# Square roots by a power instruction on GpSimd instead of ScalarE roots with Newton steps

## The chip, the cores and the metric

The kernel runs on one core of one Trainium2 chip. A core has five engines with instruction queues of their own: TensorE (matmuls; PE, and PEld for the load of its weights), VectorE (DVE), ScalarE (ACT), GpSimd (POOL) and SyncE (SP, which here only issues DMAs). They meet through semaphores. The metric is the device time of one execution in microseconds.

## The reference

Two layers over `x` (64 x 256 x 256) with one adjacency matrix `adj` (256 x 256), each a layer norm, a ReLU, a graph network and a residual sum:

```python
# layer 0
h = jnp.maximum(_layernorm(x), 0.0)
x = x + _L0_gnn_ref(h, adj, adj, W1, W2, W3)      # three products with adj*adj, widths 512, 1024, 256
# layer 1
h = jnp.maximum(_layernorm(x), 0.0)
x = x + _L1_gnn_ref(h, adj, V1, b1, V2, b2)
# inside layer 1
deg = A.sum(0) + A.sum(1) - diag(A)
d = where(deg > 0, rsqrt(deg), 0)
_, U = eigh(d[:, None] * (diag(deg) - A) * d[None, :])
out = relu((U.T @ features) @ V1 + b1) @ V2 + b2
return U @ out
```

`_layernorm` is `(x - mean) / sqrt(var + 1e-5)`. Layer 1 needs all eigenvectors of one symmetric 256 x 256 matrix, the same for the whole batch. Layer 0 doesn't depend on them.

## The kernel before, in words

**Two works at once.** The eigenvectors are one long serial chain (class `Eigen`), mostly small VectorE instructions. Layer 0 (class `Layers`) is mostly matmuls, over 32 pairs of batch entries. The kernel writes both into one program: the chain's instructions in their order, and between them, from two streams of layer-0 instructions (`products` and `rows`), whatever fits.

**The planner.** Class `Pace` decides what fits. Every call on an engine becomes an `Op`, which carries an estimate of how long it occupies its engine (`busy`, lines 107 to 120) and when its result is there (`until`). For a chain instruction, `chain` (line 211) works out when its inputs will be ready and first emits stream instructions that start before that. The order on PE and ACT is thus fixed when the program is written; a chain instruction on PE stands behind the layer-0 matmuls that the planner put in front of it, and those behind it wait if it isn't ready. Estimates of the chain are multiplied by 1.06 (1.13 in the blocks of reflections). The order on VectorE and GpSimd is left to the framework's scheduler.

**The chain's stages.** `laplacian` (402) makes the normalised matrix, with `d` from one root. `tridiagonalize` (439) takes 254 Householder steps. A step works on rows and columns from `lo` on; up to `lo` = 127 it handles two row halves of A, after that one. Each step has the same frame: `below` copies the leading entry (`alpha`) and sums the squares of the rest on ScalarE (`tail`; in the second half on VectorE); `length` (483) forms `nn` = x1*x1 + tail, takes its root `s0` on ScalarE, and forms a sign `q` and `qn`; the next step then needs `rs` = 1/s0, `qs` = q*s0, and `nb` = rs*qn + qs, which is the signed length with a Newton step on the root. `nb` (its tile is called m in the profile) goes into `ac`, whose transposes on PE (psB) start the rest of the step; `none`, made on GpSimd, goes into `den` a few instructions later. Between `nn` and `nb` VectorE updates A with two products per half (lines 559 to 561). `aside` puts single-column helpers on GpSimd in the first half and on VectorE in the second.

Then come the leaves (QL steps on 16 x 16 blocks, which keep their ScalarE roots in both versions), with the reflections put together in blocks on PE, and four levels of divide and conquer (`level`, 1280). A level takes six roots of `dq` in `rational_steps` (1189), and two with a Newton step by the helper `root` (349): of `zp` at line 1674, and of `nrm` at 1688. A root by `root` is five instructions: ScalarE Sqrt, then reciprocal, product, sum and halving on VectorE.

**The norms.** `norm` (1811) runs 65 times, for 64 half-works of a pair and once more because the first pair is split in two. Per run ScalarE sums the four parts of x, VectorE makes the mean `nm`, ScalarE sums the squares, and then VectorE (variance), ScalarE (root) and VectorE (five instructions: a Newton step, `scale`, `shift`) finish before ScalarE's `relu_norm` uses scale and shift.

**The end.** When the chain is done, a flag says whether a repair is needed (`mend`, 1726): the register read of it is followed by a branch. `go_on` puts 3.5 us of layer-0 work before it, and 4.5 us after it while layer 1's first rows load. Layer 1 (`layer1`, 2107) takes 32 items through three products each; what is left of layer 0 is filled in between its instructions, and at item 8 `finish` emits all the rest at once. The pairs 30 and 31 come as items 11 and 12. The transposes of pair 31's normed rows (`turn_rows`) are held back until item 8.

Of the kernel before, what the change touches and what calls it, by code (L numbers as in the profile page):

```python
# [27 lines left out]
N = 256  # L28
# [54 lines left out]
class Op:  # L83
# [4 lines left out]
    def __init__(self, part, call, args, kwargs):  # L88
        self.part, self.engine, self.call, self.args, self.kwargs = part, ENGINES[part], call, args, kwargs
        self.name = call.__name__  # L90
        free = lambda a: int(np.prod([int(n) for n in a.shape[1:]]))
        named = dict(kwargs)
        outs = [named.pop("out")] if "out" in named else [args[0]]
        ins = [a for a in [*(args if "out" in kwargs else args[1:]), *named.values()] if isinstance(a, bass.AP)]
        total = named.pop("accum_out", None)
        if isinstance(total, bass.AP):
            outs.append(total)
            ins = [a for a in ins if a is not total]
        self.outs, self.ins = [span(a) for a in outs], [span(a) for a in ins]
        n = max(free(a) for a in outs[:1] + ins) if self.engine == "DVE" else free(outs[0])  # L100
        sums = len(outs) > 1

        if self.engine == "PE":
            self.columns = 0 if "transpose" in self.name else n
            self.busy = max(n * self.COLUMN, 0.224) if self.columns else 0.115
            self.until = max(self.busy, 0.165) + 0.35
        elif self.engine == "ACT":
            pointers = any(isinstance(kwargs.get(k), bass.AP) for k in ("scale", "bias"))
            self.busy = 0.13 + n / 1400 + 0.12 * pointers + 0.19 * sums
            self.until = self.busy + 0.12  # L110
        elif self.engine == "DVE":
            each = 6.3 if self.name == "reciprocal" else 2.0 if self.name == "tensor_tensor_scan" else 1.0
            pointers = self.name == "scalar_tensor_tensor" or any(a.shape[1:] == [1] for a in ins[1:])
            self.busy = 0.065 + 0.06 * pointers + each * n / 960 + 0.08 * sums
            self.until = self.busy + 0.125
        elif self.engine == "POOL":
            self.busy = 0.2 + 2 * n / 960
            self.until = self.busy + 0.1
        else:
            self.busy, self.until = 0.1, 4.0  # L120
# [160 lines left out]
class Eigen:  # L281


    def __init__(self, tc, ctx, ap, gt2, pace):
# [117 lines left out]
    def laplacian(self):  # L402
# [13 lines left out]

        safe, rt, tmp = self.col("c3"), self.col("c4"), self.col("c5")
# [21 lines left out]
    def tridiagonalize(self, a):  # L439
# [24 lines left out]
        row = lambda tag: self.sp.tile([P, N], F32, tag=tag, name=tag)  # L464
        guard = self.col("guard", 1)
        nc.vector.memset(guard, 1e-30)
        book = self.mat("m1")
# [15 lines left out]
        def length(xr, lo, tail):  # L483

            nn, s0, q, qn = (self.col(c, 1) for c in ("nn", "s0", "q", "qn"))
# [5 lines left out]
            return nn, s0, q, qn  # L491

# [4 lines left out]
        alpha, tail = below(xr, 1)  # L497
        nn, s0, q, qn = length(xr, 1, tail)
        for k in range(N - 2):
# [5 lines left out]

            rs, qs, nb = self.col("rs", 1), self.col("qs", 1), nbs[:, k : k + 1]
# [56 lines left out]
            if more:  # L563
                alpha, tail, (nn, s0, q, qn) = alpha1, tail1, following

# [623 lines left out]
    def rational_steps(self, n, kd, zsum, zown, znxt, acc, s, gap, half, y, bs, rb):  # L1189
# [33 lines left out]
        for step in range(ROOT_STEPS):  # L1223
# [40 lines left out]
            self.ts(dq, dq, 1e-36, OP.max)  # L1264
            nc.scalar.activation(dq, dq, AF.Sqrt)
            self.tt(b, b, dq, OP.add)
# [13 lines left out]
    def level(self, n, qt, dc, rho, sg, bad=None):  # L1280
# [452 lines left out]
class Layers:  # L1733


    def __init__(self, tc, ctx, ap, gt2, u, ut):
# [74 lines left out]
    def norm(self, x, scale, shift, parts=range(4)):  # L1811
# [3 lines left out]
        at = slice(parts[0], parts[-1] + 1, parts[1] - parts[0])  # L1815
        s, nm, v, tmp = (self.sp.tile([P, g], F32, tag=c, name=c) for c in ("s", "nm", "v", "tmp"))
        for j in parts:
            junk = self.sp.tile([P, N], F32, tag="junk", name="junk", bufs=1)
            yield nc.scalar.activation(junk, x[:, j // 2, j % 2, :], AF.Copy, accum_out=s[:, j : j + 1])
        yield nc.vector.tensor_scalar(nm[:, at], s[:, at], -1.0 / N, None, OP.mult)  # L1820
        for j in parts:
            junk = self.sp.tile([P, N], F32, tag="junk", name="junk", bufs=1)
            yield nc.scalar.activation(
                junk, x[:, j // 2, j % 2, :], AF.Square, bias=nm[:, j : j + 1], accum_out=v[:, j : j + 1]
            )
        s, nm, v, tmp, scale, shift = (t[:, at] for t in (s, nm, v, tmp, scale, shift))
# [371 lines left out]
```

## Time and profile before

| | us |
|---|---|
| median of 3 runs (range) | 2428.49 (2427.74 to 2430.24) |
| profiled execution, span | 2426.6 |
| PE busy | 2381.5 |
| VectorE busy | 2127.2 |
| ScalarE busy | 1013.8 |
| GpSimd busy | 480.6 |
| ScalarE root of nn, 254 times | 74.5 |
| ScalarE root of v (norms), 65 times | 13.2 |
| the seven VectorE instructions of the norms, 65 times each | 78.0 |

Almost every instruction is emitted from one line of the planner (L209 in the first part, L213 after the planner's end), so groups are told apart by the tiles that they write and read and not by lines. Where the program has put several names into one place of memory, the profile shows one of them: `nb` is m, the tridiagonal form's `uc` is q, its partial products are r, `gam` is z. A matmul in 32-bit floats appears as two rows. Instructions of one engine overlap in the profile: the start of the next one, not the end of the last, tells what one costs in a chain. In the answers "idle before" is the time in which the engine stood still ahead of an instruction, with what ended it behind the arrow.

### The profile page before, as it was taken

What the parts mean: (1) busy time and instruction counts of PE and PEld (TensorE: products, weight loads), DVE (VectorE), ACT (ScalarE), POOL (GpSimd) and SP (SyncE); (2) the same over time, 40 slices, a digit from 0 to 9 for tenths busy, and PEclk for the clock granted to TensorE, in tenths of its full rate; (3) what the DMA queues carried; (4) which work ended last, traced back from release to release, by engine and by line L of the source; (5) the groups of instructions that cost most, each with busy time, mean ns of one, the idle gap of its engine ahead of it and who ended that gap; (6) DMA issues with size and microseconds to landing.
All of it is one profiled execution on the core that took longest, in us unless ns stands there. A gap on an engine that the chain in (4) does not pass through costs nothing. (4 is left out here: it accounts for less than half of the span.)

```text
span 2426.6 us, 38393 instructions
## 1 busy us (share of the span) xinstructions
PE 2381.5 (98%) x9226; PEld 1581.7 (65%) x9226; DVE 2127.2 (88%) x12971; ACT 1013.8 (42%) x2827; POOL 480.6 (20%) x1752
## 2 busy tenths in 40 slices
PE   7999999999999999999999899999999999999999
PEld 4666666666666566666666666666566666666788
DVE  8999999999999999999999989999997888886443
ACT  4444454444444444344444244344344434443322
POOL 2334333343333111111111000000000000000443
PEclk9999999999999999999999999999999999999999
DMA  3000000000000000000000000000000000000676
GB/s 113 18 21 7 23 23 18 23 23 23 6 23 23 18 22 23 22 6 23 23 23 26 10 23 23 23 23 22 18 22 27 22 23 12 16 22 1 210 255 204
DMA packets 59399, 90.02 MB, mean 37 GB/s; under 512 B 5792, under 2 KB 42784, under 8 KB 59168
## 3 DMA queue, kind: packets, MB, share of 16 engines
q1 hardware_dynamic: 59168, 87.52, 10.8%
q8 instruction: 74, 1.21, 0.2%
q14 instruction: 157, 1.29, 0.2%
HBM read 47.13 MB, written 40.37 MB: 36 GB/s over the span
## 5 line engine op out<-in xcount | busy, mean ns | idle before, releaser
L209 PE MATMUL bank<-y,L_gnn_W 128*128 128x512 f32 (+2 forms) x2182 | 903.5, 566 | 1.1 <-ACT y L209 1.1
L209 PEld LDWEIGHTS bank<-y,L_gnn_W 128*128 128x128 f32 x2182 | 401.8, 190 | 440.7 <-issue 419.0
L209 PE MATMUL bank<-L_gnn_W,s 128*128 128x256 f32 (+1 forms) x2092 | 465.2, 375 | 3.2 <-ACT s L209 3.2
L209 PEld LDWEIGHTS bank<-L_gnn_W,s 128*128 128x128 f32 x2092 | 386.7, 190 | 52.2 <-ACT s L209 3.9
L209 ACT ACTIVATE s<-bank 128x512 f32<-128x512 f32 x384 | 224.9, 586 | 196.4 <-PE bank L209 196.0
L209 PE MATMUL bank<-gt,s 128*128 128x256 f32 x1036 | 233.7, 379 | 2.8 <-ACT s L209 2.8
L209 PE MATMUL bank<-L_gnn_W,y 128*128 128x512 f32 (+2 forms) x542 | 230.9, 569 | 1.1 <-ACT y L209 1.1
L209 PEld LDWEIGHTS bank<-gt,s 128*128 128x128 f32 x1036 | 194.7, 191 | 39.7 <-issue 10.5
L209 ACT COPY y<-bank 128x512 f32<-128x512 f32 x192 | 111.5, 582 | 138.9 <-PE bank L209 138.6
L209 PEld LDWEIGHTS bank<-L_gnn_W,y 128*128 128x128 f32 x542 | 100.2, 190 | 97.3 <-issue 91.1
L209 POOL COPY m<-xr 128x1 f32<-128x1 f32 x254 | 55.8, 220 | 534.5 <-DVE xr L209 526.5
L209 ACT ACTIVATE s<-nn,guard 128x1 f32<-128x1 f32 x254 | 74.5, 293 | 208.1 <-DVE nn L209 169.0
L209 ACT ACTIVATE h<-x,shift,scale 128x256 f32<-128x256 f32 x256 | 137.3, 589 | 54.6 <-DVE shift L209 54.4
L209 ACT ACTIVATE junk<-x 128x256 f32<-128x256 f32 x256 | 105.6, 412 | 95.8 <-DVE x L209 80.5
L209 ACT ACTIVATE junk<-x,nm 128x256 f32<-128x256 f32 x256 | 129.0, 504 | 37.1 <-DVE nm L209 32.6
L209 DVE SCALAR_TENSOR_TENSOR A<-xr,wc,A 128x255 f32<-128x255 f32 (+63 forms) x381 | 139.9, 368 | 0.0
L209 DVE SCALAR_TENSOR_TENSOR A<-wr,q,A 128x255 f32<-128x255 f32 (+63 forms) x381 | 138.9, 366 | 0.0
L209 ACT ACTIVATE junk<-xr 128x254 f32<-128x254 f32 (+63 forms) x127 | 46.0, 362 | 216.5 <-DVE xr L209 211.4
L209 DVE SCALAR_TENSOR_TENSOR q<-q 128x1 f32<-128x1 f32 (+1 forms) x576 | 119.8, 208 | 13.0 <-ACT q L209 2.3
L209 PE MATMUL bank<-gt,h 128*128 128x256 f32 (+1 forms) x518 | 120.6, 382 | 0.1
L209 POOL TENSOR_TENSOR xb<-x,ub 128x512 f32<-128x512 f32 x16 | 19.9, 1271 | 495.5 <-DMA hw<-hw 485.6
L209 PE MATMUL bank<-p,gt 128*128 128x512 f32 (+2 forms) x270 | 117.0, 570 | 0.1
(615 smaller groups left out, 4306.2 us busy)
## 6 DMA issues: line engine op xcount, KB each, us to landing
x<-x SPq DMA_DIRECT2D x60, 512.0 KB, 3.6
x<-in_x_dram SPq DMA_DIRECT2D x64, 256.0 KB, 3.7
out_dram<-out SPq DMA_DIRECT2D x64, 256.0 KB, 2.2
hw<-hw SPq DMA_DIRECT2D x60, 256.0 KB, 2.7
L_gnn_W<-in_L_gnn_W_dram SPq DMA_DIRECT2D x1, 2048.0 KB, 10.9
L_gnn_W<-in_L_gnn_W_dram SPq DMA_DIRECT2D x1, 1024.0 KB, 13.5
L_gnn_W<-in_L_gnn_W_dram SPq DMA_DIRECT2D x1, 512.0 KB, 6.3
mask<-in_c_blk_dram SPq DMA_DIRECT2D x2, 256.0 KB, 3.1
```

The costliest lines, as they stand in the source:

```text
L209: return op.call(*op.args, **op.kwargs)
```

## The change

A tile of constants 0.5 and -0.5 is set once, and a helper raises a tile to that power on GpSimd. It replaces ScalarE's Sqrt and the steps around it in the front (`laplacian`), in the tridiagonal form, in `rational_steps` and at the two places in `level`; in the norms of both layers the variance, the power and the shift are all made on GpSimd, and the mean comes straight from ScalarE's scaled sum. The planner gets a price for the power. The roots in the leaves stay as they are.

```diff
         elif self.engine == "POOL":
-            self.busy = 0.2 + 2 * n / 960
+            power = OP.pow in args
+            self.busy = 0.2 + (0.14 * n + 0.15 if power else 2 * n / 960)
...
+        self.powers = {0.5: pool.tile([P, H], F32, name="half"), -0.5: pool.tile([P, H], F32, name="less")}
+        for y, t in self.powers.items():
+            tc.nc.vector.memset(t, y)
...
+    def power(self, out, a, y):
+        return self.nc.gpsimd.tensor_tensor(out, a, self.powers[y][:, 0 : out.shape[-1]], OP.pow)
...
-        self.root(rt, safe, tmp)
-        dinv = self.col("c6")
-        self.recip(dinv, rt)
+        self.power(dinv, safe, -0.5)
...
             self.stt(nn, x1, x1, tail, OP.mult, OP.add)
-            nc.scalar.activation(s0, nn, AF.Sqrt, bias=guard)
+            self.power(s0, nn, 0.5)
             aside(lo).tensor_scalar(q, x1, 0.0, 0.5, OP.is_ge, OP.subtract)
-            aside(lo).tensor_tensor(qn, q, nn, OP.mult)
...
-            self.recip(rs, s0)
-            aside(lo).tensor_tensor(qs, q, s0, OP.mult)
...
                 if h == halves[0]:
-                    self.stt(nb, rs, qn, qs, OP.mult, OP.add)
+                    self.stt(nb, q, 2.0, s0, OP.mult, OP.mult)
...
         self.ts(dq, dq, 1e-36, OP.max)
-        nc.scalar.activation(dq, dq, AF.Sqrt)
+        self.power(dq, dq, 0.5)
...
-        self.recip(zp, zp)
-        self.root(zh, zp, tmp)
+        self.power(zh, zp, -0.5)
...
-        self.root(rn, nrm, tmp)
-        self.recip(rn, rn)
+        self.power(rn, nrm, -0.5)
...
+        self.rsqrt = pool.tile([P, 2 * H], F32, name="rsqrt")
+        self.nc.vector.memset(self.rsqrt, -0.5)
...
-            yield nc.scalar.activation(junk, x[:, j // 2, j % 2, :], AF.Copy, accum_out=s[:, j : j + 1])
-        yield nc.vector.tensor_scalar(nm[:, at], s[:, at], -1.0 / N, None, OP.mult)
+            yield nc.scalar.activation(
+                junk, x[:, j // 2, j % 2, :], AF.Copy, scale=-1.0 / N, accum_out=nm[:, j : j + 1]
+            )
...
-        yield nc.vector.tensor_scalar(v, v, 0.25 / N, 0.25 * LN_EPS, OP.mult, OP.add)
-        yield nc.scalar.activation(s, v, AF.Sqrt)
-        yield nc.vector.reciprocal(tmp, s)
-        yield nc.vector.tensor_tensor(tmp, tmp, v, OP.mult)
-        yield nc.vector.tensor_tensor(s, s, tmp, OP.add)
-        yield nc.vector.reciprocal(scale, s)
-        yield nc.vector.tensor_tensor(shift, nm, scale, OP.mult)
+        yield nc.gpsimd.tensor_scalar(v, v, 1.0 / N, LN_EPS, OP.mult, OP.add)
+        yield nc.gpsimd.tensor_tensor(scale, v, self.rsqrt[:, 0 : scale.shape[-1]], OP.pow)
+        yield nc.gpsimd.tensor_tensor(shift, nm, scale, OP.mult)
```

More of the change, by code (lines that the diff above doesn't have):

```diff
@@ L415, in laplacian @@
         self.tt(deg, deg, dg, OP.subtract)
-        safe, rt, tmp = self.col("c3"), self.col("c4"), self.col("c5")
+        safe, dinv = self.col("c3"), self.col("c6")
         self.ts(safe, deg, 1e-30, OP.max)
-        self.root(rt, safe, tmp)
-        dinv = self.col("c6")
-        self.recip(dinv, rt)
+        self.power(dinv, safe, -0.5)
         self.stt(dinv, deg, 0.0, dinv, OP.is_gt, OP.mult)
@@ L464, in tridiagonalize @@
         row = lambda tag: self.sp.tile([P, N], F32, tag=tag, name=tag)
-        guard = self.col("guard", 1)
-        nc.vector.memset(guard, 1e-30)
         book = self.mat("m1")
@@ L483, in length @@
         def length(xr, lo, tail):
-            nn, s0, q, qn = (self.col(c, 1) for c in ("nn", "s0", "q", "qn"))
+            nn, s0, q = (self.col(c, 1) for c in ("nn", "s0", "q"))
             x1 = xr[:, lo : lo + 1]
             self.stt(nn, x1, x1, tail, OP.mult, OP.add)
-            nc.scalar.activation(s0, nn, AF.Sqrt, bias=guard)
+            self.power(s0, nn, 0.5)
             aside(lo).tensor_scalar(q, x1, 0.0, 0.5, OP.is_ge, OP.subtract)
-            aside(lo).tensor_tensor(qn, q, nn, OP.mult)
-            return nn, s0, q, qn
+            return nn, s0, q
         xc = self.col("xc")
@@ L497, in tridiagonalize @@
         alpha, tail = below(xr, 1)
-        nn, s0, q, qn = length(xr, 1, tail)
+        nn, s0, q = length(xr, 1, tail)
         for k in range(N - 2):
@@ L504, in tridiagonalize @@
             rc = a[:, :, lo]
-            rs, qs, nb = self.col("rs", 1), self.col("qs", 1), nbs[:, k : k + 1]
-            self.recip(rs, s0)
-            aside(lo).tensor_tensor(qs, q, s0, OP.mult)
+            nb = nbs[:, k : k + 1]
             xa, junk = self.col("xa"), self.row("r0")
@@ L563, in tridiagonalize @@
             if more:
-                alpha, tail, (nn, s0, q, qn) = alpha1, tail1, following
+                alpha, tail, (nn, s0, q) = alpha1, tail1, following
         done = slice(0, N - 2)
@@ L1264, in rational_steps @@
             self.ts(dq, dq, 1e-36, OP.max)
-            nc.scalar.activation(dq, dq, AF.Sqrt)
+            self.power(dq, dq, 0.5)
             self.tt(b, b, dq, OP.add)
@@ L1815, in norm @@
         at = slice(parts[0], parts[-1] + 1, parts[1] - parts[0])
-        s, nm, v, tmp = (self.sp.tile([P, g], F32, tag=c, name=c) for c in ("s", "nm", "v", "tmp"))
-        for j in parts:
-            junk = self.sp.tile([P, N], F32, tag="junk", name="junk", bufs=1)
-            yield nc.scalar.activation(junk, x[:, j // 2, j % 2, :], AF.Copy, accum_out=s[:, j : j + 1])
-        yield nc.vector.tensor_scalar(nm[:, at], s[:, at], -1.0 / N, None, OP.mult)
+        nm, v = (self.sp.tile([P, g], F32, tag=c, name=c) for c in ("nm", "v"))
         for j in parts:
@@ L1823, in norm @@
             yield nc.scalar.activation(
-                junk, x[:, j // 2, j % 2, :], AF.Square, bias=nm[:, j : j + 1], accum_out=v[:, j : j + 1]
+                junk, x[:, j // 2, j % 2, :], AF.Copy, scale=-1.0 / N, accum_out=nm[:, j : j + 1]
             )
-        s, nm, v, tmp, scale, shift = (t[:, at] for t in (s, nm, v, tmp, scale, shift))
-        yield nc.vector.tensor_scalar(v, v, 0.25 / N, 0.25 * LN_EPS, OP.mult, OP.add)
-        yield nc.scalar.activation(s, v, AF.Sqrt)
-        yield nc.vector.reciprocal(tmp, s)
-        yield nc.vector.tensor_tensor(tmp, tmp, v, OP.mult)
-        yield nc.vector.tensor_tensor(s, s, tmp, OP.add)
-        yield nc.vector.reciprocal(scale, s)
-        yield nc.vector.tensor_tensor(shift, nm, scale, OP.mult)
+        for j in parts:
+            junk = self.sp.tile([P, N], F32, tag="junk", name="junk", bufs=1)
+            yield nc.scalar.activation(
+                junk,
+                x[:, j // 2, j % 2, :],
+                AF.Square,
+                bias=nm[:, j : j + 1],
+                accum_out=v[:, j : j + 1],
+            )
+        nm, v, scale, shift = (t[:, at] for t in (nm, v, scale, shift))
+        yield nc.gpsimd.tensor_scalar(v, v, 1.0 / N, LN_EPS, OP.mult, OP.add)
+        yield nc.gpsimd.tensor_tensor(scale, v, self.rsqrt[:, 0 : scale.shape[-1]], OP.pow)
+        yield nc.gpsimd.tensor_tensor(shift, nm, scale, OP.mult)
     def relu_norm(self, x, scale, shift, h, parts=range(4)):
```

## The prediction

> **What bounds the kernel now.** The page first: the span, the busy shares, and the chain that ended last.
>
> ```profile
> span 2426.6 us, 38393 instructions
> PE 2381.5 (98%) x9226; PEld 1581.7 (65%) x9226; DVE 2127.2 (88%) x12971; ACT 1013.8 (42%) x2827; POOL 480.6 (20%) x1752
> PE 7%; DVE 0%; ACT 0%; issue 0%; ACTq 0%; DVEq 0%
> ```
>
> TensorE is busy 98% of the span. The chain of waits names 7% only, since it breaks off where the flag is read; the rest must come from stages. The view of busy time by stage, cut where the work changes (columns: PE, PEld, DVE, ACT, POOL busy, then clock, DMA share, GB/s):
>
> ```profile
> 0.00:20.00 20.00, 8.56 (x23) 5.51 (x24) 10.45 (x63) 9.85 (x29) 1.81 (x10) 1.00 0.92 307
> 20.00:1322.00 1302.00, 1291.02 (x5083) 839.23 (x5082) 1250.31 (x7895) 590.43 (x1711) 391.66 (x1645) 1.00 0.06 20
> 1322.00:1390.00 68.00, 58.82 (x289) 46.56 (x288) 61.67 (x400) 14.98 (x34) 0.45 (x2) 0.97 0.05 16
> 1390.00:2240.00 850.00, 843.98 (x3011) 535.82 (x3009) 730.72 (x4505) 350.66 (x963) 6.76 (x31) 1.00 0.06 20
> 2240.00:2256.00 16.00, 13.31 (x51) 9.01 (x50) 4.75 (x10) 4.40 (x14) 2.87 (x3) 1.00 0.42 148
> 2256.00:2427.00 171.00, 165.77 (x776) 145.51 (x776) 69.26 (x101) 43.49 (x78) 77.04 (x62) 1.00 0.67 224
> ```
>
> Row two is the tridiagonal form: VectorE is busy 96% and TensorE 99%, at once. Row four (leaves and levels) keeps TensorE at 99% with VectorE at 86%. Busy matmuls are modelled, so I checked by columns: 24 matmuls of 256 columns take 5.13 us in the timeline at 506 us, 1,198 columns per us. All matmul rows kept apart by shape hold 2.825 million columns: 2354 us at 1,200 per us. **Only 72 us of the span are not matmul columns**: some 20 at the start, 13 between 1300 and 1400 (the blocked reflections), 6 between 2200 and 2300, 4 at the end, 29 spread thinly. The change removes no matmul, so it can win only out of these.
>
> The second fact is where layer 0 ends. The eigenvectors' chain on VectorE gives its last wide result at 2235 us; the last products of pair 31 run at 2247 to 2249, and what follows is layer 1. **Both queues of work run out together.** A shorter chain leaves layer 0's matmuls to be done afterwards, at the same cost; a longer one leaves TensorE with nothing to fill. The chain is worth nothing when shortened and its full length when lengthened.
>
> The third is the coupling. TensorE's order is fixed when the program is written, by the planner's estimate of the chain. In 20 to 1322 us TensorE waits for VectorE at the chain's transposes (psB) 7.6 us in 15 of 254 steps, VectorE for them 6.5 us in 22 (the views of waits). If a step gets shorter by less than the planner thinks, TensorE waits at every transpose and that time is lost.
>
> **Part by part.** How one step's root stands now, in the second half of the steps (timeline, VectorE alone):
>
> ```profile
> 1002.67 0.21 DVE L209 SCALAR_TENSOR_TENSOR nn<-xr,m 128x1 f32<-128x1 f32 x1
> 1002.81 0.15 DVE L209 TENSOR_TENSOR xc<-xc,lower 128x1 f32<-128x1 f32 x1
> 1002.88 0.29 DVE L209 SCALAR_TENSOR_TENSOR A<-wr,q,A 128x80 f32<-128x80 f32 x1
> 1003.09 0.15 DVE L209 TENSOR_TENSOR qn<-q,nn 128x1 f32<-128x1 f32 x1
> 1003.21 0.30 DVE L209 SCALAR_TENSOR_TENSOR A<-xr,wc,A 128x80 f32<-128x80 f32 x1
> 1003.42 0.16 DVE L209 RECIPROCAL rs<-s 128x1 f32<-128x1 f32 x1
> 1003.50 0.14 DVE L209 TENSOR_TENSOR qs<-q,s 128x1 f32<-128x1 f32 x1
> 1003.55 0.23 DVE L209 SCALAR_TENSOR_TENSOR r<-A,xr 128x79 f32<-128x79 f32 x1
> 1003.71 0.08 DVE L209 DVE_READ_ACCUMULATOR r<-A,xr 128x1 f32 x1
> 1003.71 0.22 DVE L209 SCALAR_TENSOR_TENSOR m<-rs,qn,qs 128x1 f32<-128x1 f32 x1
> ```
>
> *The price of a power.* No row has one. It cannot be cheaper than a POOL product of one column (gg, 195 ns beside little, qs 375 ns beside the updates of A); from above I allow 1 us, where a step's cover ends (below). I take 0.5 us for one column, nearer to the product's rows than to the upper end, and for wider ones the slope that the diff writes into the planner, 0.14 us a column: 0.63 for two, 0.9 for four. The slope is the code's claim and no measurement; few powers are wide, so little hangs on it.
>
> *Second half (127 steps).* qn, rs and qs go: starts of 0.12, 0.08 and 0.05 us, 0.25 together. nn ends at 1002.88; a power of 0.5 from 1002.93 ends at 1003.43, and m could start at 1003.46, where VectorE arrives. Early steps gain up to 0.25; in the last ones (1309 us) nn to m takes 0.85 us with narrow updates between, which no longer cover the power, and they gain nothing. Average 0.1: 13 us.
>
> *First half (127 steps).* rs goes (0.08), and so does the wait for qs: at 504 us m starts at 504.89 because POOL ends qs at 504.86, while VectorE was free at 504.71. The power starts near 503.66 and, even stretched to 0.75 us, ends before 504.63, where m then stands. `none`, queued behind it on POOL and needed by den at 505.0, just fits. 0.26 x 127 = 33 us. What hides the power is the four updates of A, 0.31 us each; a power above 1 us would lose that cover.
>
> *Norms (65).* Seven VectorE instructions go, 78.0 us busy and about 26 us of waits (v 13.2, nm 9.7, tmp 3.5); back to back they fill about half their length, so some 60 us of the chain. POOL gets three, about 0.25 + 0.91 + 0.2 = 1.4 us each time, in order with the tridiagonal helpers; the first waits for ScalarE's sums, and alpha, `none` and the power of a step would wait behind it. VectorE does the same waiting today, so I charge nothing net.
>
> *Levels and front.* 24 roots of dq: rb waited 26.9 us for them, 1.1 each; a power of 0.63 plus hops is 0.8: 7 us. Eight roots with Newton steps: 1.2 us each (2226.06 to 2227.16) become 0.75: 4 us. In the front, c waits 10.23 to 11.90 for root and steps; a power of 0.63 ends near 10.85, so psC starts 0.8 us sooner; the first h waits for v, power and shift until about 12.1 in place of 12.45. Start: 0.7 us.
>
> *Two memsets and 94 us less on ScalarE* (254 x 293, 65 x 206 ns and the small ones) cost and bring nothing: ScalarE is 42% busy.
>
> The chain is thus some 33 + 13 + 60 + 7 + 4 = 117 us shorter on VectorE. **Hardly any of it reaches the end.** What does: the start, 0.7; about half of TensorE's 7.6 us at the transposes, 3.5, since VectorE now runs ahead of the plan by the norms' time; and the gap at 2240 to 2256, where TensorE is idle 2.7 us while flag and first rows arrive, which left-over layer-0 products now fill. Sum 6.9. Span 2426.6 - 6.9 = 2419.7; the median of the runs lies 1.9 us above the profiled span, so **2421.6 us**.
>
> **The rule that speaks against it.** The Trainium skill (SBUF — State Buffer, Who interferes with whom) says that a GpSimd instruction that reads SBUF and a VectorE instruction with two SBUF inputs take one port pair in turn, the later one fully blocked for the whole instruction of the other. The trace shows it where POOL's instruction is long: under xb (1.27 us), v takes 1067 ns against a median of 164. Small ones hardly block: gc takes 0.26 us where gg runs beside it and 0.21 elsewhere; updates of A are at most 0.01 longer beside a POOL instruction. By the row a power costs VectorE 0.05 us a step, 13 us in all, less than is removed; by the rule it holds the pair for its 0.5, some 127 us over 254 steps, more than is removed. A power reads one column and computes; I take the row, and keep the rule as a rival.
>
> **Rivals.**
>
> *The power holds the port.* Place: between nn and m in each step, before an update of A. Price: the 0.3 us by which it exceeds a product, plus 0.05. First half 0.35 - 0.08 = 0.27 x 127 = 34 us, second half 0.35 - 0.25 = 0.10 x 127 = 13 us. The planner knows nothing of it, so TensorE waits: 2421.6 + 47 = **2468 us**. It decides from a hold of about 0.13 us on. For it: xb's row and the rule; against it: gg and the A rows.
>
> *The last pair is caught in the open.* Layer 1's first eight items put about one waiting layer-0 product before each of their own some 84, at about 0.55 us on average 46 us, plus the two fills of 3.5 and 4.5. If more than some 50 us are left when the chain ends, pair 31's norm falls at the end of the forced finish, where TensorE has nothing else: 2.5 us of squares, 1.1 of copies, 1.7 on POOL, 2.1 of relu and 0.8 for the addition are 8 us idle: 2421.6 + 8 = **2430 us**. Today the norm is hidden beside layer 1 (its transposes start at 2290.70 with no gap).
>
> *The chain was the bound after all.* Then its time counts down to the columns plus the start and tail, about **2385 us**. Against it: 99% busy TensorE through 850 us of levels.
>
> *The order comes out differently*, or a first power waits for something that no row shows: about 2440.
>
> **Numbers.** Forecast 0.45, last pair 0.20, port 0.27, chain 0.03, order 0.05. A measurement of this kernel tells 0.2%, 4.9 us, from no change; the forecast is 6.9 away, so 0.35 of its 0.45 are faster and 0.10 same. Faster: 0.35 + 0.03 = 0.38. Same: 0.10 + 0.18 = 0.28. Slower: 0.34. The range takes the forecast with its 10 us of scatter and most of the port's cost: 2411 to 2466; the likeliest case alone, 2414 to 2428.
>
> **What would show it.** Right: matmul columns unchanged; the levels end some 50 to 100 us sooner; TensorE's waits for xr and ac at psB fall to near nothing; layer-0 products stand among the layer-1 ones after the flag; powers of 0.4 to 0.6 us. Wrong: updates of A lengthened by 0.3 us beside a power (port); psB waits in most of the 254 steps (plan); an idle TensorE of 8 us before the last transposes of h (last pair). A power above 1 us would overturn the forecast.

## The result, and the profile after

| | before | after |
|---|---|---|
| median (range), us | 2428.58 (2427.74 to 2430.24) | 2439.59 (2437.77 to 2443.25) |
| ratio, 95% interval | | 1.0048 [1.0036, 1.0060] |
| span of the profiled execution | 2426.6 | 2436.2 |

The change makes the kernel 0.5% slower. VectorE has 110 us less to do and ScalarE 73 us less, and TensorE's matmuls are the same. First the page of the changed kernel: its span, the busy time of each engine, and the chain that ended last.

```profile
span 2436.2 us, 36959 instructions
...
PE 2382.1 (98%) x9216; PEld 1579.2 (65%) x9216; DVE 2016.9 (83%) x11965; ACT 941.0 (39%) x2475; POOL 672.0 (28%) x1980
...
PE 8%; DVE 0%; ACT 0%; issue 0%; ACTq 0%
```

As before, the chain of waits breaks off where the flag is read and decides nothing. Next the changed kernel by stage, with the cuts that the prediction used (busy time of PE, PEld, DVE, ACT, POOL, then clock, DMA share and GB/s).

```profile
0.00:20.00 20.00, 8.55 (x24) 5.22 (x24) 8.95 (x50) 9.95 (x28) 4.52 (x15) 1.00 0.92 308
20.00:1322.00 1302.00, 1277.91 (x5047) 833.51 (x5046) 1175.48 (x7172) 514.11 (x1389) 516.96 (x1753) 1.00 0.06 20
1322.00:1390.00 68.00, 61.40 (x273) 42.29 (x272) 63.68 (x444) 22.86 (x62) 3.59 (x9) 1.00 0.04 12
1390.00:2240.00 850.00, 842.79 (x2985) 532.48 (x2984) 701.35 (x4203) 344.23 (x906) 65.91 (x137) 1.00 0.06 21
2240.00:2256.00 16.00, 16.00 (x75) 12.92 (x74) 1.38 (x2) 3.79 (x7) 9.87 (x8) 1.00 0.64 240
```

In the tridiagonal form (row two) TensorE is busy 1277.9 us where it was 1291.0, although VectorE has 75 us less to do there. The gap around 2240 us is filled: TensorE is busy 16.00 of 16.00 us where it was 13.31.

**Lost time by stage.** The matmul rows, summed over the whole span by shape, hold 2,798,338 columns in both kernels: 2331.9 us at the prediction's rate of 1,200 a microsecond. TensorE thus spends 94.7 us without columns before and 104.3 after, and this 9.6 us is the whole difference of the spans. The same sum for each stage, its length less its columns, gives the table on which the rest stands. (Matmuls at a cut count on both sides, so a row adds up to some 3 us too little.) "First" is 20 to 760 us, "second" from there to the last step, "reflections" up to the first leaf, then leaves and levels up to the flag.

| lost us | start | first | second | reflections | leaves, levels | end |
|---|---|---|---|---|---|---|
| before | 14.7 | 21.1 | 14.2 | 8.0 | 22.9 | 10.8 |
| after | 14.2 | 24.3 | **27.5** | 4.9 | 22.2 | 7.9 |
| e2_norms_back | 13.8 | 16.8 | 22.3 | 6.6 | **32.7** | 8.8 |
| e3_steps_back | 15.1 | 23.6 | 13.6 | 5.6 | 20.9 | 7.8 |
| e9_order | 14.7 | 25.1 | 20.6 | 4.9 | 22.2 | 7.9 |
| e12_order_norms | 13.5 | 17.2 | 13.4 | 6.0 | **34.0** | 9.1 |
| e13_norms_by_stage | 14.2 | 17.2 | 13.8 | 6.0 | 19.4 | 7.6 |
| e15_stage_steps_back | 13.6 | 20.4 | 14.4 | 8.3 | 22.0 | 13.6 |

The change loses 13 us in the second half of the steps and 3 in the first, and wins 6 in the reflections and at the end.

A stop of TensorE can cost more than its own length. In some places its granted clock stands at half for 3.4 us after one, and this counts as lost time too (1.7 us each). From the reflections to the end of the kernel there are two such stretches before the change (at 1344 and 1716 us) and one after it (at 1944 us), so 1.7 of the 6 us won are one stretch less. There is none in the steps in any of the kernels.

**What happens in a step.** The waits of the changed kernel between 740 and 1322 us, for VectorE and then for TensorE (total us, times, longest):

```profile
DVE m L210 <- POOL s L210: 68.8, 126, 2.1
DVE r L210 <- PE psB L210: 2.9, 10, 0.4
```

```profile
PE psB L210 <- DVE xr L210: 9.9, 14, 1.5
PE psB L210 <- DVE ac L210: 3.0, 4, 1.2
```

VectorE waits for the power (s) in 126 of some 130 steps, 0.53 us a step over 130. Before, the largest wait of VectorE here was 1.6 us, and TensorE waited 1.4 and 1.2 at psB for the same two:

```profile
DVE r L209 <- PE psB L209: 1.6, 8, 0.3
```

```profile
PE psB L209 <- DVE ac L209: 1.4, 2, 1.0
PE psB L209 <- DVE xr L209: 1.2, 3, 0.6
```

The timeline of the changed kernel, VectorE and GpSimd, over the place that the prediction showed of before (start, length):

```profile
1002.58 0.22 DVE L210 SCALAR_TENSOR_TENSOR nn<-xr,m 128x1 f32<-128x1 f32 x1
...
1002.78 0.29 DVE L210 SCALAR_TENSOR_TENSOR A<-wr,q,A 128x76 f32<-128x76 f32 x1
1002.90 0.60 POOL L210 TENSOR_TENSOR s<-nn,half 128x1 f32<-128x1 f32 x1
...
1003.53 0.16 DVE L210 SCALAR_TENSOR_TENSOR m<-q,s 128x1 f32<-128x1 f32 x1 [0.46 <-POOL s L210]
1003.61 0.29 DVE L210 SCALAR_TENSOR_TENSOR A<-xr,wc,A 128x76 f32<-128x76 f32 x1
1003.81 0.21 DVE L210 SCALAR_TENSOR_TENSOR den<-m,none 128x1 f32<-128x1 f32 x1
1003.94 0.23 DVE L210 SCALAR_TENSOR_TENSOR r<-A,xr 128x75 f32<-128x75 f32 x1
...
1004.29 0.21 DVE L210 SCALAR_TENSOR_TENSOR ac<-A,m,xa 128x1 f32<-128x1 f32 x1
```

Before, m stood behind r. The framework, which orders VectorE, now puts it ahead of the second update of A, where the power is not done: VectorE stands still 0.46 us, and A, den, r and the reciprocal are still to come before ac. From the start of nn to that of ac the median in the second half is 1.71 us, and was 1.29.

The plan on TensorE doesn't know it. By the planner's own clock, printed while the program is written, steps 130 to 250 take 4.33 us each before and 4.25 after; by the traces they take 4.35 and 4.39. TensorE's share between two transposes was cut by 0.08 us a step, and the step did not get shorter: it runs over its plan by 0.14 us where it was 0.02, and 0.12 more in each of 127 steps is 15 us, near the 13.3 of the table.

### The profile page after: what moved, and what is told of

It is laid out like the page before. It is cut to its first block, busy times and chain, and to the rows that moved or that the text cites. A ratio compares the mean times of both kernels' runs of the same rounds, so it can differ in the third digit from the quotient of the medians.

```text
span 2436.2 us, 36959 instructions
## 1 busy us (share of the span) xinstructions
PE 2382.1 (98%) x9216; PEld 1579.2 (65%) x9216; DVE 2016.9 (83%) x11965; ACT 941.0 (39%) x2475; POOL 672.0 (28%) x1980
## 3 DMA queue, kind: packets, MB, share of 16 engines
q1 hardware_dynamic: 59168, 87.52, 10.7%
q8 instruction: 74, 1.21, 0.2%
## 5 line engine op out<-in xcount | busy, mean ns | idle before, releaser
L210 PE MATMUL bank<-y,L_gnn_W 128*128 128x512 f32 (+3 forms) x2188 | 908.9, 566 | 2.1 <-DVE x L210 1.9
L210 PE MATMUL bank<-L_gnn_W,s 128*128 128x256 f32 x2084 | 464.3, 376 | 0.0
L210 PE MATMUL bank<-gt,s 128*128 128x256 f32 (+1 forms) x1038 | 231.9, 377 | 1.6 <-ACT s L210 1.5
L210 PEld LDWEIGHTS bank<-gt,s 128*128 128x128 f32 x1038 | 193.4, 190 | 39.7 <-issue 12.7
L210 POOL TENSOR_TENSOR s<-nn,half 128x1 f32<-128x1 f32 x254 | 161.9, 637 | 19.9
L210 ACT COPY p<-bank 128x512 f32<-128x512 f32 x64 | 37.3, 582 | 245.7 <-PE bank L210 245.7
## 6 DMA issues: line engine op xcount, KB each, us to landing
L_gnn_W<-in_L_gnn_W_dram SPq DMA_DIRECT2D x1, 2048.0 KB, 10.7
```

The costliest lines, as they stand in the source:

```text
L210: return op.call(*op.args, **op.kwargs)
```

## The experiments

All are edits of the changed kernel, timed beside the kernel before (medians of 2427.4 to 2428.4 us); the ratios are to it.

**The planner's price.**

```diff
-            self.busy = 0.2 + (0.14 * n + 0.15 if power else 2 * n / 960)
+            self.busy = 0.2 + (0.13 * n + 0.3 if power else 2 * n / 960)
```

> The changed kernel with one line altered: the planner books a power at 0.2 + 0.13 a column + 0.3, so 0.63 us for one column where the trace has 0.637 (it booked 0.49). Plan theory (the planner thinks a tridiagonal step shorter than it is, puts too little layer-0 work between two transposes, and TensorE waits): the lost columns of the second half of the steps fall from 27 us to about 15, and the time to 2425 to 2431 us. Queue theory (norm instructions on GpSimd block the powers) and level theory (roots of dq are dearer as powers): nothing of that changes, 2436 to 2441 us.

Measured: 2438.61 (2434.17 to 2440.84), ratio 1.0049 [1.0035, 1.0062]. A power booked nearer to its measured price changes the median by 1 us, where the plan theory expected 9 to 15. The profiled run is the fastest of the five (2434.17). In it the second half loses 20.4 in place of 27.5, not the 15 that was expected, and start and end lose 4.6 more (16.4 and 10.3). The price is not the cure.

**Which part of the change costs.** Three runs take one part back each: `norm` (e2), `tridiagonalize` (e3), and `rational_steps` with the two roots of `level` (e4), all written as before. The core of e3's edit (the norm's is the change's own diff turned round, the levels' is shown with e10):

```diff
-            self.power(s0, nn, 0.5)
+            nc.scalar.activation(s0, nn, AF.Sqrt, bias=guard)
...
+            self.recip(rs, s0)
+            aside(lo).tensor_tensor(qs, q, s0, OP.mult)
...
-                    self.stt(nb, q, 2.0, s0, OP.mult, OP.mult)
+                    self.stt(nb, rs, qn, qs, OP.mult, OP.add)
```

> The changed kernel with the norms as before (VectorE and ScalarE). Queue theory: the powers of the steps are no longer stopped by norm instructions that wait for ScalarE, 2425 to 2431 us. Plan theory: VectorE gets 455 instructions back, the steps get longer still, and the time stays or grows, 2438 to 2450 us. Level theory: 2437 to 2441.

> The changed kernel with the tridiagonal form as before (root on ScalarE, rs, qn, qs), the rest by powers. Plan theory and queue theory alike: the steps are as fast as before or faster by the norms' VectorE time, 2420 to 2430 us. Level theory: the loss is in the levels, so 2434 to 2440 us.

> The changed kernel with the roots of the levels as before (ScalarE, and Newton steps for zp and nrm). Level theory: the levels lose 14.3 us of columns after and 6.9 before, so 7 us come back, 2430 to 2434 us. Plan and queue theory: 2436 to 2441 us.

Measured: e2 2437.29, 1.0040 [1.0027, 1.0054]; e3 **2422.51** (2421.08 to 2424.8), 0.9980 [0.9972, 0.9988]; e4 2436.59, 1.0036 [1.0023, 1.0050]. The steps hold the whole loss: with them as before the rest of the change is worth 5 us, near what the prediction gave to the change as a whole. The norms look harmless in e2, but the table shows two large terms that cancel: 12.7 us less lost in the steps, 10.5 more in leaves and levels.

**The plan's length of a step.** The factor 1.06 on the chain's estimates, in the second half only:

```diff
             rc = a[:, :, lo]
+            self.pace.slower = 1.1 if lo >= P else self.pace.SLOWER
```

> The changed kernel, where the planner stretches its estimates by 1.10 in place of 1.06 in the second half of the steps, and nowhere else. Plan theory (TensorE's fixed order holds too little layer-0 work between two transposes, because steps are planned 0.10 to 0.25 us shorter than they run): the columns lost there fall from 27 us to 13 to 20, and the time to 2426 to 2434 us. Latency theory (the power is simply longer than the root and stands on the chain, whatever the order): the lost time stays, 2437 to 2444 us.

> The same factor at 1.02. Plan theory: the planned steps shrink by 0.04 of some 4.1 us, 0.16 us x 127 = 20 us more of TensorE's time is lost there, 45 to 50 us in all, and the kernel takes 2450 to 2462 us. Latency theory: 2437 to 2444 us as before.

Measured: with 1.1, 2430.96 (2428.08 to 2434.21), 1.0014 [1.0007, 1.0020]; with 1.02, 2442.55, 1.0061 [1.0047, 1.0075]. More room in TensorE's order wins back 8.6 us (second half lost 21.6; another 3.7 us less are lost between the steps and the flag, of which 1.7 are the half-clock stretch, absent here), less room costs 3 (30.5). The direction is the plan theory's. The second size misses: 2450 to 2462 us and 45 to 50 us of lost time were expected. With the shorter plan the second half is itself shorter, 545.9 us in place of 557.0, so the chain waits for TensorE's order too.

**Half of the steps, and none.** e7 has ScalarE's root in the second half alone; e8 has powers in the norms and the front alone (e3's and e10's edits together). The core of e7's:

```diff
-            self.power(s0, nn, 0.5)
+            if lo < P:
+                self.power(s0, nn, 0.5)
+            else:
+                nc.scalar.activation(s0, nn, AF.Sqrt, bias=guard)
```

> The changed kernel with the root, rs, qs, qn of the second half of the steps as before (ScalarE), the power kept in the first half, the norms, the levels and the front. If the loss sits in the second half alone, as its lost columns say: 2418 to 2425 us, like the kernel with all steps as before. If the first half's powers lose too: 2428 to 2434 us.

> The changed kernel with steps and levels as before: only norms and front by powers. If the gain of the kernel with its steps as before (2422.5 us) comes from the norms, 2419 to 2425 us; if the levels share in it, 2425 to 2429 us.

Measured: e7 2423.01 (2421.44 to 2423.83), 0.9981 [0.9973, 0.9989]; e8 2423.90 (2421.89 to 2425.92), 0.9984 [0.9978, 0.9991]. The loss is in the second half of the steps (13.6 us lost there in e7, 14.2 before). Powers in the first half bring nothing beside e3 (2422.51), as long as norms stand in GpSimd's queue: the first half loses 23.8 us in e7 and 23.6 in e3.

**VectorE's order.** Is it the power, or the place where its result is asked for? The framework can be told to queue nb behind the product that gives xa. TensorE's order and the planner's estimates don't change by this.

```diff
-                self.stt(junk[:, r], a[:, h, r], 1.0, xr[:, r], OP.mult, OP.mult, accum=xa[:, h : h + 1])
-                if h == halves[0]:
+                total = self.stt(junk[:, r], a[:, h, r], 1.0, xr[:, r], OP.mult, OP.mult, accum=xa[:, h : h + 1])
+                if h == halves[0] and lo < P:
                     self.stt(nb, q, 2.0, s0, OP.mult, OP.mult)
+                elif h == halves[0]:
+                    with self.tc.issue_after(total.ins):
+                        self.stt(nb, q, 2.0, s0, OP.mult, OP.mult)
```

> All of the change, and in the second half of the steps (lo >= 128) nb is queued on VectorE behind the product that gives xa, so that both updates of A and that product stand beside the power; in the changed kernel the framework puts nb ahead of the second update of A, where VectorE waits 68.8 us for s in 126 of 127 steps. TensorE's order and the planner's estimates stay as in the changed kernel. Theory (the uncovered wait for the power is what makes the steps longer than the plan): VectorE's wait for s between 740 us and the end of the steps falls from 68.8 us to below 25 us, TensorE's lost time there from 27.5 us to 13 to 18, and the time from 2439 to 2423 to 2428. Rival (TensorE loses for another reason, such as GpSimd's part in the loop by itself or contention): the wait falls and TensorE's loss stays above 23, time 2435 to 2442. Second rival (the power holds VectorE up wherever it stands): the wait moves behind the product and stays above 50 us.

Measured: 2431.93 (2429.02 to 2433.81), 1.0021 [1.0013, 1.0028]. In its timeline the power is covered:

```profile
1000.44 0.21 DVE L210 SCALAR_TENSOR_TENSOR nn<-xr,m 128x1 f32<-128x1 f32 x1
...
1000.64 0.29 DVE L210 SCALAR_TENSOR_TENSOR A<-wr,q,A 128x76 f32<-128x76 f32 x1
1000.97 0.30 DVE L210 SCALAR_TENSOR_TENSOR A<-xr,wc,A 128x76 f32<-128x76 f32 x1
1001.30 0.24 DVE L210 SCALAR_TENSOR_TENSOR r<-A,xr 128x75 f32<-128x75 f32 x1
1001.46 0.08 DVE L210 DVE_READ_ACCUMULATOR r<-A,xr 128x1 f32 x1
1001.46 0.15 DVE L210 SCALAR_TENSOR_TENSOR m<-q,s 128x1 f32<-128x1 f32 x1
1001.65 0.22 DVE L210 SCALAR_TENSOR_TENSOR ac<-A,m,xa 128x1 f32<-128x1 f32 x1
```

Beside the two updates GpSimd works at the power, which ends at 1001.36, before m starts:

```profile
1000.76 0.60 POOL L210 TENSOR_TENSOR s<-nn,half 128x1 f32<-128x1 f32 x1
```

From nn to ac it is 1.21 us, 0.50 less than in the changed kernel, and m follows without a wait. VectorE's and TensorE's waits of this kernel from 740 to 1322 us:

```profile
DVE m L210 <- POOL s L210: 10.7, 13, 1.6
```

```profile
PE psB L210 <- DVE xr L210: 7.8, 13, 1.1
```

The wait fell from 68.8 to 10.7 us, as expected. The time fell by 7.7 us, about half of what was expected, and the lost time of the second half to 20.6, not to 13 to 18; the kernel is still slower than before. 13 steps still wait. One of them, the timelines of GpSimd, VectorE and TensorE in the same kernel:

```profile
827.08 0.20 POOL L210 TENSOR_SCALAR v<-v 128x4 f32<-128x4 f32 x1 [1.89 <-ACT junk L210]
827.36 1.03 POOL L210 TENSOR_TENSOR scale<-v,rsqrt 128x4 f32<-128x4 f32 x1
828.47 0.20 POOL L210 TENSOR_TENSOR shift<-nm,scale 128x4 f32<-128x4 f32 x1
828.61 0.28 POOL L210 COPY m<-xr 128x1 f32<-128x1 f32 x1
828.97 0.23 POOL L210 TENSOR_SCALAR none<-m 128x1 f32<-128x1 f32 x1
829.28 0.56 POOL L210 TENSOR_TENSOR s<-nn,half 128x1 f32<-128x1 f32 x1
```

```profile
829.88 0.16 DVE L210 SCALAR_TENSOR_TENSOR m<-q,s 128x1 f32<-128x1 f32 x1 [1.03 <-POOL s L210]
```

```profile
830.43 0.29 PE L210 MATMUL psB<-ident,ac 128*128 128x128 f32 x1 [0.72 <-DVE xr L210]
```

A norm's v waits 1.89 us for ScalarE's sums at the head of GpSimd's queue, its power takes 1.03, and behind it stand alpha (m<-xr), none and the step's own power. VectorE waits 1.03 us for that one, and TensorE 0.72 at psB.

**Levels, with the order mended, and with half of the steps.** Both have `rational_steps` and the two roots of `level` as before; e10 on top of e9, e11 on top of e7.

```diff
-        self.power(dq, dq, 0.5)
+        nc.scalar.activation(dq, dq, AF.Sqrt)
...
-        self.power(zh, zp, -0.5)
+        self.recip(zp, zp)
+        self.root(zh, zp, tmp)
```

> As e9_order, and rational_steps and the two roots in level as before. Theory: the levels' powers are worth some 1 to 3 us on the wrong side in the changed kernel (e4_levels_back), so 2420 to 2426, at most 3 us below e9_order. Rival: the levels are neutral once the steps are mended, within 1.5 us of e9_order.

> ScalarE's root in the second half of the steps and in the levels, powers in the first half, the norms and the front. Theory (only the uncovered power of the second half costs; levels cost 1 to 3): 2420 to 2423, at or a little below e7_first_half's 2423.0. Rival (levels neutral or a gain): 2423 to 2426.

Measured: e10 2430.73 (2428.96 to 2433.92), 1.0014 [1.0006, 1.0023], 1.2 us below e9; e11 2423.52 (2421.77 to 2425.03), 0.9984 [0.9977, 0.9990], 0.5 us above e7. The 3.0 us that e4 lies below the changed kernel don't come again, and e4's trace lacks that kernel's half-clock stretch of 1.7 us. The levels' powers are worth nothing that these runs can tell.

**The norms out of GpSimd's queue.** e9 with `norm` as before:

```diff
...
-        yield nc.gpsimd.tensor_tensor(scale, v, self.rsqrt[:, 0 : scale.shape[-1]], OP.pow)
...
+        yield nc.scalar.activation(s, v, AF.Sqrt)
+        yield nc.vector.reciprocal(tmp, s)
...
```

> As e9_order (nb behind the product of xa in the second half), and norm as before, so that no four-column power (1.02 us) and no wait for ScalarE's sums stands in GpSimd's queue ahead of a step's power. In e9_order VectorE still waits 10.7 us for s in 13 steps of the second half, each some 2 us behind a norm's power, and TensorE waits 7.8 us at psB in 13 steps, nearly the same ones. Theory (what was left in e9_order is the norms' place in GpSimd's queue): VectorE's wait for s in the second half below 2 us, TensorE's at psB below 3 us, TensorE's lost time there from 20.6 to 13 to 17 us, and the time from 2432 to 2423 to 2428. Rival (the loss left in e9_order is not the queue's, and the norms' VectorE instructions take back what GpSimd gives free): 2430 to 2434, as e2_norms_back stood only 2 us below the changed kernel.

Measured: 2429.35 (2428.34 to 2430.49), 1.0006 [0.9998, 1.0014]. The step's theory holds in the steps: VectorE's wait for s in the second half is 0.5 us, TensorE's at psB 2.6, and 13.4 us are lost where it was 20.6. The time moves by 2.6 us only, and 2423 to 2428 were expected: leaves and levels lose 34.0 us where e9 lost 22.2. ScalarE's timeline in this kernel at a norm among the leaves, and TensorE's waits between 1338 and 1731 us:

```profile
1671.39 0.57 ACT L210 ACTIVATE s<-bank 128x512 f32<-128x512 f32 x1
1674.81 0.20 ACT L210 ACTIVATE s<-v 128x4 f32<-128x4 f32 x1 [2.85 <-DVE v L210]
1677.28 1.09 ACT L210 ACTIVATE h<-x,shift,scale 128x256 f32<-128x256 f32 x2 [2.26 <-DVE shift L210]
1678.27 0.57 ACT L210 ACTIVATE s<-bank 128x512 f32<-128x512 f32 x1
```

```profile
PE bank L210 <- ACT s L210: 6.8, 2, 4.6
```

ScalarE's order is fixed too. The norm's root waits 2.85 us there for v, which VectorE does between its own chain instructions, and h waits 2.26 us more for shift; s<-bank, a ReLU of layer 0, is queued behind both, and TensorE stands still 4.6 us for it. With the norm on GpSimd one of these two waits is gone. From 1340 to 2250 us TensorE waits 9.0 us for s in e12 and 0.7 in e9.

**Half a clock behind the stop.** TensorE at this stop, and the 7 us behind it by engine:

```profile
1678.90 7.30 PE L210 MATMUL bank<-L_gnn_W,s 128*128 128x256 f32 x21 [4.56 <-ACT s L210]
```

```profile
1677.00:1684.00 7.00, 5.10 (x12) 4.11 (x13) 6.66 (x63) 4.22 (x10) 0.00 (x0) 0.51 0.01 2
```

The granted clock is 0.51 there, and the products of 256 columns start 0.427 us apart, where they start 0.216 apart from 1684 us on. Of leaves and levels e12 spends 17.1 us at half clock in four stretches, e9 3.4 in one. At half speed 8.5 and 1.7 us of that are lost, so 6.8 of the 11.8 us between the two kernels are the clock, and the rest is about what TensorE's waits there grew by (10.7 to 16.2 us).

**The norms by stage.** So beside the steps' powers the norms on GpSimd cost in the steps, and in e12 their lack costs afterwards. e13 is e9 with the norms that are written during the steps as before, and those after them by power (`norm_steps` is `norm` as before; the second place in the diff stands behind the last step); e14 has besides the levels as before; e15 has these norms, and the steps as before.

```diff
+        if self.pace.steps:
+            yield from self.norm_steps(x, scale, shift, parts)
+            return
...
+        self.pace.steps = False
         done = slice(0, N - 2)
```

> As e9_order (nb behind the product of xa), and the norms written during the tridiagonal steps as before (ScalarE root, VectorE), those written after them by power on GpSimd. Theory (the norms on GpSimd cost in the steps, where its queue holds a step's power, and pay in leaves and levels): lost time of TensorE 17 us in the first half, 13 to 15 in the second, 20 to 24 in leaves and levels, 14 + 5 + 8 elsewhere, about 80 us over 2331.9 us of columns: span 2410 to 2415, time 2412 to 2418. Rival (the loss only moves): leaves and levels lose over 28 us and the time is 2422 to 2430.

> As e13_norms_by_stage, with rational_steps and the two roots of level as before. Theory (the levels' powers cost 1 to 3 us): 2410 to 2416, below e13. Rival (neutral): within 1.5 us of e13.

> The changed kernel with tridiagonalize as before, and the norms written during the steps as before, those after them by power. Theory (the norms' place decides, and the steps as before lose 21 and 14 us as in the kernel before): leaves and levels 20 to 22 us, span 2414 to 2419, time 2416 to 2421, some 3 us above e13 since powers in the first half spare 4 us there. Rival (norms by power in the steps do no harm where the steps have no power, as e3_steps_back's first half lost 23.6 and its second 13.6): 2421 to 2424.

Measured: e13 **2415.26** (2414.45 to 2417.36), 0.9947 [0.9933, 0.9960]; e14 2415.28 (2414.35 to 2415.94), 0.9946 [0.9932, 0.9960]; e15 2431.17 (2429.01 to 2433.14), 1.0012 [1.0003, 1.0021]. e13 and e14 are faster than both kernels and in the range that was expected, nearly so stage by stage as well; that e14 stands level with e13 says again that the levels' powers are neutral. e15 missed its range by 10 us, and the rival's by 7: its leaves and levels lose 22.0 as expected, its reflections 8.3 and its end 13.6. The stage from 1390 to the flag and the 16 us behind the flag, in e13; then the 16 us behind the flag in e15:

```profile
1390.00:2221.00 831.00, 825.29 (x2933) 522.53 (x2932) 692.95 (x4151) 337.74 (x893) 72.54 (x136) 1.00 0.06 20
2221.00:2237.00 16.00, 15.85 (x82) 13.88 (x81) 1.99 (x4) 2.02 (x4) 6.64 (x6) 1.00 0.69 247
```

```profile
2243.00:2259.00 16.00, 11.57 (x37) 7.61 (x38) 4.19 (x9) 6.88 (x21) 5.64 (x7) 0.89 0.59 213
```

e15's chain ends at 2243.2 us, as before (2243.0), with no layer-0 product left to fill the place: TensorE is busy 11.57 of 16 us behind the flag. It stands still for 4.28 us, and 3.4 us at half clock follow (the mean clock of the row is 0.89). e13's ends at 2220.6, and layer-0 products fill that place, 15.85 of 16. That explains 6 us of the 10; some 2 more are in the reflections, where e15 has a half-clock stretch at 1343 us, as before, and e13 has none. e15's median also lies 1.3 us above its profiled run of 2429.89, which stays open.

That powers pay after the steps is not shown in general. The kernel before, with its norms on VectorE and ScalarE, loses 22.9 us in leaves and levels, and e15, with powers there, 22.0. So the 34.0 of e12 depend on where the fixed order puts the same norms; why they stop TensorE there and not in the kernel before was not tested.

## Why the prediction was wrong

It forecast 2421.6 us and named faster the likeliest; the kernel is at 2439.59 and slower. Most of its steps stand. Two that decided failed, and together they carried the sign: the cover of the power in the second half of the steps, and the norms in GpSimd's queue. In the second half the change loses 27.5 us; with the first mended it loses 20.6 (e9), with the second 22.3 (e2), with both 13.4 (e12), and before it was 14.2. Each alone leaves the kernel slower than before (e9 1.0021, and e2 1.0040, which also loses in the leaves and levels). With both mended where they cost (e13) it wins 13.1 us, nearly twice the 6.9 that were forecast for the change.

- **"Only 72 us of the span are not matmul columns"**: 94.7. The 2.825 million columns counted matmuls twice at the edges of the windows from which they were added up (windows of 50 us give this sum); the sum over the whole span is 2.798 million. That the matmuls don't change, and that only the rest is to be won, holds.
- **The first failed step: "Second half (127 steps)" and what reaches the end from it.** Three terms of it fell.
  - *The gain.* "Starts of 0.12, 0.08 and 0.05 us, 0.25 together" was read as time that a step gets back. The second update of A needs the first, and r needs the second. In the second half the starts of the two updates are 0.32 us apart (median) in before, with 1.3 other instructions between them, and 0.32 apart in e9, with 0.1 between. qn, rs and qs stood in gaps that stay when they go. From nn to ac e9 saves 0.08 us a step, not up to 0.25.
  - *The cover.* "m could start at 1003.46, where VectorE arrives" took for granted that m stays behind r. The framework puts it ahead of the second update, and the power, 0.60 us here where 0.5 was forecast, isn't done: 68.8 us of waiting. The prediction's own reading, "TensorE waits at every transpose and that time is lost", named this danger; the sum put it at nothing. With m in its old place (e9) the same power is covered, and 7.7 us of time come back.
  - *TensorE's waits at psB.* "About half of TensorE's 7.6 us at the transposes" was to come back. They grew from 7.1 us for xr and ac (0.5 more was for another tile) to 21.1; from 20 to 1322 us, first before and then after:

```profile
PE psB L209 <- DVE xr L209: 3.9, 8, 1.0
PE psB L209 <- DVE ac L209: 3.2, 6, 1.1
```

```profile
PE psB L210 <- DVE xr L210: 18.1, 24, 1.5
PE psB L210 <- DVE ac L210: 3.0, 4, 1.2
```

- **The second failed step: "I charge nothing net" for the norms in GpSimd's queue.** The cost was some 15 us, and its danger had been written down: "alpha, `none` and the power of a step would wait behind it". VectorE did the same work before, but a norm there takes its turn between chain instructions when its inputs are ready; at the head of GpSimd's queue it waits for ScalarE with a step's power behind it. From e9 to e13, which differ in the norms of the steps alone, the first half loses 25.1 and then 17.2 us, the second 20.6 and then 13.8. In the first half (20 to 740 us) VectorE's wait for s falls from 15.0 us in 28 steps to 3.4 in 19.
- **The first half's 33 us of chain.** The power, 0.68 us here, is covered by the four updates as the prediction argued, apart from the steps behind a norm. With norms in GpSimd's queue it brings no time (e7 against e3); without them the first half loses 17.2 us where it loses 20.4 with ScalarE's root (e13 against e15).
- **The chain's end "50 to 100 us sooner"**: 11.6 (2231.4 in place of 2243.0). The chain waits for TensorE's order (e6), so what VectorE saves doesn't run ahead. But what is won at the end did come as written: the gap of 2240 to 2256 is filled, and the end loses 2.9 us less.
- **The size of the rest.** With the steps as before the kernel stands at 2422.5; the forecast of 2421.6 was the change without the loss in its steps. That the two agree is in part luck: in e3's trace the end wins 3.0 us, near the 2.7 of the sum, but the steps lose 1.9 more than before, where 3.5 were to be won, and reflections, leaves and levels win 4.4, to which the sum gave nothing.
- **Rivals.** *Port*: its time, 2468, was wrong, and no update of A is held up in its place. The updates of A start 0.32 us apart with a power beside them (e9) as with ScalarE's root beside them (before); the Trainium skill's rule (SBUF — State Buffer, Who interferes with whom) isn't borne out for a power of one column, as the row had said. The row itself, v under xb, is an instruction with one input; of two-input ones under the same sums tmp takes 0.73 and s 1.19 us where 0.16 is usual, so there the rule is borne out. *Last pair*: no wait of such a size; the longest of TensorE behind the flag is 0.6 us. (Before, the pair's transposes start at 2289.10; the row at 2290.70 is the product behind them, after a wait of 0.57.) *Chain was the bound*: no. *The order comes out differently*, with "about 2440" and a chance of 0.05, is half of what happened: VectorE's order, where the prediction had thought of none in particular. Its time fits by luck, since it stood for no sum.

## What to carry to other kernels

Instructions that stand in the gap between two dependent ones cost nothing, and removing them brings nothing (the updates of A start 0.32 us apart with 1.3 instructions between them and with 0.1): see from which result the next long one waits before a start-to-start distance is counted as a gain. When a result moves to an engine with a longer latency, ask who decides where it is asked for: a scheduler can put its reader where it isn't there yet (why it did so here isn't shown), and one order edge may be worth more than the new instruction. Side work in an in-order queue belongs where nothing urgent stands behind it, and that can differ from stage to stage: beside the steps' powers the norms on GpSimd cost about 15 us (e9 against e13), beside ScalarE's roots 2.4 (the steps in e3 against e15), and after the steps they spared 14.6 of lost time in one pair of kernels (e12 against e13) and 0.9 in another (before against e15). When TensorE stops, look at the granted clock behind the stop before the stop alone is charged.

## What the runs showed of the hardware

The groups of the changed kernel on GpSimd for the powers of one, four and two columns (count, busy us, mean ns, idle before):

```profile
L210 POOL TENSOR_TENSOR s<-nn,half 128x1 f32<-128x1 f32 x254 | 161.9, 637 | 19.9
L210 POOL TENSOR_TENSOR scale<-v,rsqrt 128x4 f32<-128x4 f32 x63 | 64.9, 1031 | 5.1
...
L210 POOL TENSOR_TENSOR rdq<-rdq,half 128x2 f32<-128x2 f32 x24 | 16.7, 696 | 254.6 <-DVE rdq L210 254.6
```

A power takes 0.64, 0.70 and 1.03 us for one, two and four columns. A line from one column to four would be 0.5 us and 0.13 a column (an estimate from these means); a product of one column (gg) takes 0.19. Powers of one column take 0.68 us on average in the first half of the steps and 0.59 in the second; whether the wider updates beside them hold them up isn't shown.

A two-input VectorE update beside a power is not held up. In the changed kernel 17 updates of A lie wholly inside a four-column power of 1.03 us, and none is over 0.005 us longer than the median of its width. Under 128x512 sums of GpSimd (1.27 us), before, five small VectorE instructions (nm, v, tmp, s, shift) did take 0.6 to 1.0 us longer; v is the one that the prediction showed. So what holds VectorE up here is not the length of GpSimd's instruction alone; which property it is stays open.

TensorE ran at half clock for 3.4 or 6.8 us behind some of its stops, most of them 1.9 to 4.6 us long; behind others of up to 3.0 us it did not. What decides isn't shown here.
